# Sharing out the filler work over the four key tiles of a causal attention quad, and one staging tile of V for each layer

## The chip, the cores and the metric

The kernel runs on one core of one Trainium2 chip. The metric is the time of one execution on the device in microseconds (us); the time of a kernel is the median of several runs. A trace of one further, profiled execution shows what each engine did: TensorE (PE, with its weight loads as PEld), VectorE (DVE), ScalarE (ACT), GpSimd (POOL), and SyncE (SP), which only issues DMAs.

## The reference

Sixteen sequences (batches) of 512 tokens with 256 channels go through four attention layers, each with a layer norm ahead of it and a residual sum behind it. All have 16 heads of 16 channels. Layer 0 is causal attention with biases, layer 2 is attention with rotary positions, and layers 1 and 3 (the same weights twice) are attention in which tokens are split into two groups by a similarity; the split needs the minimum and maximum over all batches.

```python
def _L0_attn_a_ref(x, Wq, bq, Wk, bk, Wv, bv, Wo, bo):
    Q = x @ Wq.T + bq
    ...
    scores = jnp.einsum('bhqd,bhkd->bhqk', Qh, Kh) / jnp.sqrt(jnp.float32(HEAD_DIM))
    mask = idxs[None, :] <= idxs[:, None]
    scores = jnp.where(mask[None, None], scores, jnp.float32(-10000.0))
    attn = jax.nn.softmax(scores, axis=-1)
    ...
x = x + _L0_attn_a_ref(_layernorm(x, axis=-1), ...)
x = x + _L0_ffn_ref(_layernorm(x, axis=-1), ...)
x = x + _L0_attn_b_ref(_layernorm(x, axis=-1), ...)
x = x + _L0_ffn_ref(_layernorm(x, axis=-1), ...)
```

## The kernel before

**Tiling.** The work goes layer by layer (`PLAN`, line 62: causal "a", split "f", rotary "b", split "f"), in a layer batch by batch, in a batch by four *quads* of four heads (`quads`, line 587). A quad has four *key tiles* t = 0 to 3 of 128 keys. Queries and keys of a quad are read from HBM into one of five pairs of buffers (`load_quad`, line 574).

For one key tile PE makes the transposed scores (`products.score`, line 678: matmuls of line 687, and in the causal layer eight mask matmuls of line 698), ACT takes their exponentials (line 702), and PE multiplies them with V (`weigh`, line 706). In the causal layer a key tile t meets only the queries from 128 t on, so the scores are 512, 384, 256 and 128 columns wide for t = 0 to 3. Tiles 0 and 1 are the two *wide* ones: four exponentials each. In the narrow tiles 2 and 3 two score matrices share a bank of PSUM, and two exponentials do.

Some 20 half tiles ahead (`AHEAD`, line 63, `advance`, line 1056), the row maxima of a later quad are made: PE makes the scores once more (`maxima.score`, line 601, matmuls of line 610), and DVE takes their maxima (line 626). In the causal layer query tile t has 128 (t + 1) keys. As 20 half tiles are two quads and two tiles, the maxima of query tiles 2 and 3 (384 and 512 wide) stand beside key tiles 0 and 1, and those of query tiles 0 and 1 (128 and 256) beside key tiles 2 and 3.

**The other work.** Everything else is cut into steps, held in a list (`fill`) and put between the key tiles by a planner that runs when the kernel is built. The steps of layer 0's stretch are: `prep` of layer 0 for the batch after next (line 300; below called P: two normalizing steps n0 and n1, two steps v0 and v1 that make V, and q0, q1, k0, k1), the sums that a fully masked head needs (`masked`, line 836; m0 to m3), `tail` of the batch before (line 871; four divisions d0 to d3, two turns, two projections), and `prep` of layer 1 for batches whose tail is done (F: n0, n1, v0, v1, q0, q1, k0, `similar`, k1, `similarity`). A step has a planned cost on PE in ns (450 for a normalizing, dividing or turning step, 1380 for V and a projection, 1362 for q or k, 1750 for `similar`, 920 or 460 for `masked`) and a time before which it isn't due.

**How the order is set.** The order of PE's instructions is written out by hand: it is the order in which the planner emits them. The other engines' instructions are ordered by a scheduler; each engine and each DMA queue then works in its order and waits on semaphores. Each key tile (loop in line 1107) brings a fixed ration of planned time, `RATE` (line 1023), in `fill_in` (line 1026); `drain` (line 1006) takes the first step that is due and allowed, as long as the step costs no more than twice the credit in hand, and the credit is capped. At the third quad of a batch a `drain` without a credit (line 1095) runs whatever is needed until the batch before has been divided; at the end of a layer everything that is left is run (line 1127), because the split of the next layer needs all batches.

**V.** The steps v0 and v1 write the two halves of one of two staging tiles, `vst[b % 2]` (line 458), and a DMA on SP's queue sends the tile to HBM (line 482), from where `load_values` (line 581) reads it one layer later in the order of work. A flag lets only one `prep` of a layer at a time be past its normalizing steps (line 498), while one of layer 0 and one of layer 1 may run side by side.

Of the kernel before, what the change touches and what calls it, by code (L numbers as in the profile page):

```python
# [119 lines left out]
def hybrid_kernel(ctx: ExitStack, tc: tile.TileContext, a: dict, out: bass.AP):  # L120
# [24 lines left out]
    def small(name, dtype=F32):  # L145
        return ps_x.tile([P, S], dtype, tag="x", name=name)
# [84 lines left out]
    vst = []  # L231
    for i in range(2):
        t = res.tile([P, NT, VW], F32, tag=f"vst{i}", name=f"vst{i}")
# [3 lines left out]
    for i in range(2):  # L237
        t = res.tile([P, RW], FR, tag=f"rst{i}", name=f"rst{i}")
# [61 lines left out]
    def prep(layer, b, x):  # L300
# [154 lines left out]

        def values(u):

            v = vst[b % 2]
            xh, xl = st["xh"], st["xl"]
            ps = small(f"pv{n}_{u}")  # L460
            for k in range(2):
                t = 2 * u + k
                ts = slice(t * P, (t + 1) * P)
                seq = [(xl, wh), (xh, wl), (xh, wh)]
                for q, (xx, ww) in enumerate(seq):
                    for c in range(2):
                        nc.tensor.matmul(  # L467
                            ps[:, k * C : (k + 1) * C],
                            xx[:, c, ts],
                            ww[:, c, WV, :],  # L470
                            start=(q == 0 and c == 0),
                            stop=(q == 2 and c == 1),
                        )
            vo = v[:, 2 * u : 2 * u + 2, 0 : H * HV].rearrange("p t (h e) -> p t h e", e=HV)[:, :, :, 0:D]
            vi = ps.rearrange("p (t h d) -> p t h d", t=2, d=D)
            if kind == "a":
                bias = bv.rearrange("p (h d) -> p h d", d=D).unsqueeze(1).to_broadcast([P, 2, H, D])
                nc.vector.tensor_tensor(vo, vi, bias, ALU.add)
            else:
                nc.scalar.copy(vo, vi)  # L480
            if u == 1:
                nc.sync.dma_start(vd[b], v)
# [98 lines left out]
    def load_values(layer, b):  # L581
        t = p2.tile([P, NT, VW], F32, tag="v", name=f"v{layer}_{b}")
        nc.sync.dma_start(t, vd[b])
        V[layer, b] = t
# [251 lines left out]
    def masked(b):  # L836

        v = V[0, b]
        w_ = slice(0, H * HV)
        st = {}  # L840

        def start():
            nc.scalar.activation(EX[b], EX[b], AF.Exp)
            wv = p1.tile([P, 2, H * HV], F32, tag="wv", name=f"wv{b}")
            nc.gpsimd.tensor_tensor(wv[:, 1, :], v[:, 2, w_], v[:, 3, w_], ALU.add)
            nc.gpsimd.tensor_tensor(wv[:, 0, :], v[:, 1, w_], wv[:, 1, :], ALU.add)
            st["wv"] = wv
            X[b] = p1.tile([P, NT, H, HV], F32, tag="extra", name=f"xt{b}")

        def tile_(t):  # L850
            pf = small(f"sf{b}_{t}")
            nc.tensor.matmul(pf[:, w_], late["later"], v[:, t, w_], start=True, stop=(t == NT - 1))
            if t < NT - 1:
                rest = v[:, 3, w_] if t == 2 else st["wv"][:, t, :]
                nc.tensor.matmul(pf[:, w_], ones, rest, start=False, stop=True)
            nc.vector.tensor_tensor(
                X[b][:, t],
                pf[:, w_].rearrange("p (h e) -> p h e", e=HV),
                EX[b][:, t, :].unsqueeze(2).to_broadcast([P, H, HV]),
                ALU.mult,  # L860
            )

        yield (lambda: (b == 0 or (0, b - 1) in divided) and NG * b + NG - 1 in put), 0
        start()
        for t in range(NT):
            yield (POOL if t == 0 else 0), (460 if t == NT - 1 else 920)
            tile_(t)
        summed.add(b)
# [122 lines left out]
    def push(gen, rank):  # L991

        k = sum(s.rank <= rank for s in fill)
        fill.insert(k, Steps(gen, rank))
# [4 lines left out]
    def push_call(f, after=None):  # L999
        def gen():  # L1000
            yield (lambda: busy["prep"] == 0 and (not after or after in tailed)), 0
            f()

        push(gen(), 1)

    def drain(credit=None, until=None):

        while fill and not (until and until()):
            now = clock["now"]
            able = [s for s in fill if s.ready <= now and (s.next == 0 or banks[0] <= now) and s.open()]  # L1010
            if not able:
                if credit is not None:
                    return
                clock["now"] = min(max(s.ready, banks[0] if s.next else 0) for s in fill if s.open())
                continue
            s = able[0]
            if credit is not None:
                if s.next > 2 * max(0, credit["ns"]):
                    return
                credit["ns"] -= s.next  # L1020
            s.run()

    RATE = {0: 2100, 1: 1350, 2: 1250, 3: 700}
    credit = {"ns": 0}

    def fill_in(layer):

        credit["ns"] = min(credit["ns"] + RATE[layer], 2 * RATE[layer])
        drain(credit)

    def load_through(i):
        while loaded["n"] <= min(i, len(quads) - 1):
            j = loaded["n"]
            layer, b, g = quads[j]
            if (layer, b) not in prepared:
                drain(until=lambda: (layer, b) in prepared)
            if j >= NB:
                l_, b_, g_ = quads[j - NB]
                if PLAN[l_] == "f":
                    drain(until=lambda: (l_, b_, g_ // 2) in registered)  # L1040
            load_quad(j)
            loaded["n"] += 1

    def prep0(b, x=None):
        push(prep(0, b, load_x(0, b) if x is None else x), 2)
        busy["first"] += 1
        constant_rows(b)
# [27 lines left out]
    for i, (layer, b, g) in enumerate(quads):  # L1075
        kind = PLAN[layer]
        alone = b == 0 and g == 0 and (layer == 0 or kind == "f")
        held = kind != "f" and layer + 1 < len(PLAN) and PLAN[layer + 1] == "f"
        end = (layer + 1) * B * NG if held else len(quads)
        if b or g or layer:  # L1080
            load_through(min(end - 1, i + 4))
        if g == 0:
            load_values(layer, b)
            if kind == "f":
                first, second = registers(layer, b)
                push(first, 2)
                push(second, 2)
        if layer == 0 and g == (1 if b == 0 else 0):
            if b == 0:
                push_call(late_constants)  # L1090
            if b + 2 < B:
                prep0(b + 2)
        if g == 2 and i > NG:
            before = (layer, b - 1) if b else (layer - 1, B - 1)
            drain(until=lambda: before in divided)
        if kind == "a" and g == 1:
            push(masked(b), 2)
        if b == 0 and g == NG - 1 and layer + 1 < len(PLAN):
            push_call(lambda layer=layer: W.__setitem__(layer + 1, load_weights(layer + 1, False)))
        if b == 0 and g == NG - 2:  # L1100
            push_call(lambda layer=layer: WP.__setitem__(layer, load_weights(layer, True)), layer and (layer - 1, B - 1))
        if alone:
            advance((2 * NT) * i + AHEAD, 900)
        if i not in put:
            drain(until=lambda: i in put)
        score, weigh = products(i)
        for t in range(NT):
            for p in range(2):
                advance(min(2 * (NT * i + t) + p + 1 + AHEAD, 2 * NT * end))
                score(t, p)  # L1110
                clock["now"] += 230 + TURN
                if p == 0:
                    fill_in(layer)
                elif waiting:
                    waiting()
                    clock["now"] += 868 + TURN
                    waiting = None
            if t == 0 and g == 0 and (b > 0 or (layer > 0 and kind != "f")):
                push_tail(*((layer, b - 1) if b else (layer - 1, B - 1)))
            if i == 0:  # L1120
                load_through(i + 4) if t == NT - 1 else None
            waiting = lambda weigh=weigh, t=t: weigh(t)
        if kind != "f" and b == B - 1 and g == NG - 1 and layer + 1 < len(PLAN):
            waiting()
            waiting = None
            push_tail(layer, b)
            drain()
            split(layer + 1)
# [46 lines left out]
```

## Time and profile before

| | |
|---|---|
| median of 3 runs | 4260.31 us (4257.6 to 4260.97) |
| the profiled execution's own time | 4242.52 us |
| its span, first to last instruction | 4240.7 us |
| PE, DVE, ACT, POOL busy | 93%, 76%, 62%, 43% of the span |
| granted clock of PE, mean | 0.946 |
| first causal product / first product of layer 1 | 100.4 us / 1381.7 us |

A page of the profile gives, by part: (1) the busy time of each engine, (2) the span in 40 equal slices with the busy share of each engine in tenths and the clock that PE was granted, (3) DMA queues, (4) the chain of work that ended last, (5) the costliest groups of instructions with their mean time, and the idle time of the engine ahead of them with what ended it, (6) DMA issues. "L687" is line 687 of the kernel. The trace can also be asked for the busy times of all engines in chosen stretches, for who waited for whom, and for the instructions in order of time. A busy PE is not a PE at its peak: matmuls overlap, and short waits for a bank of PSUM disappear in their modelled ends.

### The profile page before, as it was taken

The page shows a single profiled execution, that of the slowest core. Times are in us where ns is not written, and L with a number is a line of the kernel's source. Part 1 is how long each engine was busy: PE and PEld are TensorE (multiplying, and loading weights), DVE is VectorE, ACT ScalarE, POOL GpSimd, SP SyncE. Part 2 cuts the span into 40 slices and gives each one's busy share as a digit, 9 for nine tenths or more (in the row PEclk, how much of TensorE's full clock was granted, in tenths as well). Part 3 has the DMA queues.
Part 4 walks back from the last instruction along what each step waited for, and adds up shares of the span by engine and source line. Part 5 has one row for each costly group of instructions (what it writes and reads, how often), then busy time and mean ns, then how long its engine had stood idle before and what let it go on. Part 6 is the DMA issues. An engine that isn't in the chain of part 4 may idle for free.

```text
span 4240.7 us, 79626 instructions
## 1 busy us (share of the span) xinstructions
PE 3937.4 (93%) x27440; PEld 2051.1 (48%) x27440; DVE 3207.0 (76%) x7488; ACT 2631.8 (62%) x5288; POOL 1820.8 (43%) x2421
## 2 busy tenths in 40 slices
PE   3899999999995999999999999999999599999999
PEld 2565656565553444444444444444444334444444
DVE  4676776667654888888888788888886389999996
ACT  1444454444452777777777667777777267777777
POOL 2124545354543256656665634444444412222221
PEclk6899999899996999999999999999999689999999
DMA  9556566666645345555554645455554623333331
GB/s 300 160 159 187 182 200 181 189 184 190 193 128 167 96 137 170 163 149 165 171 162 152 186 146 169 146 167 168 164 157 126 188 85 114 122 116 114 119 121 51
DMA packets 294722, 661.84 MB, mean 156 GB/s; under 512 B 51624, under 2 KB 90032, under 8 KB 294320
## 3 DMA queue, kind: packets, MB, share of 16 engines
q1 hardware_dynamic: 204080, 384.02, 28.9%
q0 software_dynamic: 90240, 272.73, 21.6%
q8 instruction: 219, 3.59, 0.3%
q14 instruction: 183, 1.50, 0.1%
HBM read 379.46 MB, written 298.06 MB: 160 GB/s over the span
## 4 chain that ended last, share of the span: by engine, by line
PE 72%; DVE 10%; DMA 7%; SPq 3%; ACT 3%; issue 3%; POOL 2%; ACTq 0%; DVEq 0%; POOLq 0%
PE po L713 19%; PE s L610 15%; PE t L687 11%; DVE mx L619 5%; PE pv L467 5%; PE pj L922 4%; PE pq L360 4%; DMA qd<-tq 3%; PE pk L360 3%; PE ot L884 2%; POOL nd L432 2%; DVE sc L626 1%; PE rs L759 1%; PE t L698 1%; SPq L568 1%
## 5 line engine op out<-in xcount | busy, mean ns | idle before, releaser
L702 ACT ACTIVATE e<-t 128x512 f32<-128x512 f32 (+2 forms) x3840 | 2017.6, 588 | 824.2 <-PE t L687 538.6
L619 DVE TENSOR_REDUCE mx<-s 128x1 f32<-128x512 f32 x3072 | 1944.4, 681 | 334.7 <-PE s L610 326.2
L610 PE MATMUL s<-ks,qs 52*128 52x512 f32 (+4 forms) x4096 | 1030.8, 481 | 92.3 <-DMA ks<-kd 78.1
L687 PE MATMUL t<-qs,ks 52*128 52x512 f32 (+4 forms) x4096 | 1000.2, 402 | 103.5 <-ACT e L702 35.5
L713 PE MATMUL po<-e,v 128*32 128x512 f32 (+1 forms) x8192 | 1031.1, 576 | 5.1 <-ACT o L729 3.9
L610 PEld LDWEIGHTS s<-ks,qs 48*128 48x128 f32 (+1 forms) x4096 | 429.9, 191 | 1085.7 <-ACT e L702 310.9
L687 PEld LDWEIGHTS t<-qs,ks 50*128 50x128 f32 (+1 forms) x4096 | 496.8, 191 | 302.3 <-DVE mx L619 102.6
L626 DVE CUSTOM_DVE_ANT_0 sc<-s,mask_s_bf 128x128 bf16<-128x128 f32 (+3 forms) x1024 | 497.7, 486 | 160.5 <-PE s L610 78.6
L577 POOL DMA_DIRECT2D qs<-qd x256 | 153.6, 601 | 811.5 <-PE t L687 530.7
L657 POOL DMA_DIRECT2D qs<-md x512 | 268.5, 529 | 543.7 <-DMA md<-ms 516.2
L432 POOL TENSOR_TENSOR nd<-nd,nhalf 128x16 f32<-128x16 f32 x120 | 346.1, 2902 | 22.5 <-DVE nd L423 22.5
L713 PEld LDWEIGHTS po<-e,v 128*32 128x32 f32 x8192 | 162.6, 109 | 271.9 <-issue 194.3
L309 POOL TENSOR_SCALAR xn<-x,nm,st 128x256 f32<-128x256 f32 x256 | 141.4, 557 | 117.7 <-PE xp L340 111.1
L698 PE MATMUL t<-mask_t_bf 64*128 64x128 bf16 x2048 | 189.4, 234 | 0.0
L380 POOL CAST tq<-yq 128x512 fp32r<-128x512 f32 x80 | 49.1, 613 | 267.9 <-DMA qd<-tq 92.5
L884 PE MATMUL ot<-ident,o 128*128 128x128 f32 x1024 | 148.2, 288 | 16.3 <-DVE tq L399 7.1
L577 POOL DMA_DIRECT2D ks<-kd x256 | 140.1, 548 | 52.1 <-issue 14.5
L729 ACT COPY o<-po 128x512 f32<-128x512 f32 x256 | 153.3, 599 | 7.4 <-PE po L713 7.0
L884 PEld LDWEIGHTS ot<-ident,o 128*128 128x128 f32 x1024 | 117.1, 146 | 47.8 <-DVE mx L619 10.1
L340 PE MATMUL xp<-ident,xn 128*128 128x128 f32 x512 | 89.1, 299 | 46.0 <-POOL xn L309 43.7
L930 DVE TENSOR_TENSOR x<-pj,x 128x512 f32<-128x512 f32 x128 | 87.1, 680 | 55.0 <-PE pj L922 50.5
L347 ACT CAST xh<-xp 128x512 fp32r<-128x512 f32 x128 | 76.0, 595 | 84.1 <-PE xp L340 83.9
(358 smaller groups left out, 4991.6 us busy)
## 6 DMA issues: line engine op xcount, KB each, us to landing
qs<-qd POOLq DMA_DIRECT2D x256, 512.0 KB, 4.5
ks<-kd POOLq DMA_DIRECT2D x256, 512.0 KB, 5.3
qd<-tq SPq DMA_DIRECT2D x256, 256.0 KB
kd<-tk SPq DMA_DIRECT2D x256, 256.0 KB
vd<-vst SPq DMA_DIRECT2D x64, 576.0 KB
v<-vd SPq DMA_DIRECT2D x64, 576.0 KB
qd<-tq SPq DMA_DIRECT2D x256, 128.0 KB
kd<-tk SPq DMA_DIRECT2D x256, 128.0 KB
```

The source lines that it names most:

```text
L360: nc.tensor.matmul(dst, ww[:, c, w, cols], xx[:, c, :], start=(k == 0 and c == 0), stop=(k == 2 and c == 1))
L432: nc.gpsimd.tensor_tensor(nd[:, 0, t], nd[:, 0, t], nhalf[:, t], ALU.pow)
L577: nc.gpsimd.dma_start(t, d[:, :, 2 * g : 2 * g + 2, :].rearrange("e r h s -> (e r) h s"))
L610: nc.tensor.matmul(st["ps"][e][:, (p % m) * end :][:, :end], q[r, p, t * P : (t + 1) * P], k[r, p, :end], start=True, stop=True,)
L619: nc.vector.tensor_reduce(st["mx"][:, e, p, t : t + 1], st["ps"][e], AX.X, ALU.max, negate=True)
L626: nc.vector.tensor_tensor_reduce(w, st["ps"][e][:, (i % m) * end :][:, :end], late["mask_s"][:, S - end :], 1.0, -3.0e38, ALU.add, ALU.max ...
L657: nc.gpsimd.dma_start(q[r : r + 2], d[:, e].rearrange("k j t p -> k j (t p)"))
L687: nc.tensor.matmul(ps[e], k[rows[e], p, t * P : (t + 1) * P], q[rows[e], p, q0:], start=True, stop=(kind != "a"),)
L698: nc.tensor.matmul(ps[e][:, :P], mk[:, 0], mk[:, 1], start=False, stop=(o == 1))
L702: st["exp", t] = nc.scalar.activation(e_[:, : m * w], st["ps"][e][:, : m * w], AF.Exp)
L713: mm = nc.tensor.matmul(st["po"][32 * j : 32 * j + 32, q0:], v[:, t, h * HV : h * HV + 32], E.pop((t, j)), start=(t == 0), stop=(t == NT - 1),
L884: nc.tensor.transpose(ps[:, g * P : (g + 1) * P], O[layer, b, g][:, t * P : (t + 1) * P], ident)
```

## The change

The ration of a key tile in layer 0 was 2100 for all four tiles; it becomes 1400 for the two wide ones and 2800 for the two narrow ones, which is 8400 for a quad as before. The cap on the credit is written in another way: what is left over is cut to one ration of the tile at hand before that ration is added. For equal rations (layers 1 to 3) this is the same as before. In layer 0 it cuts what is left to 1400 at a wide tile and to 2800 at a narrow one, where it was 2100.

The staging tile of V is chosen by layer and no longer by batch: all of layer 0's `prep` (and layer 2's) write the first tile, and all of layer 1's (and layer 3's) the second.

```diff
@@ values, line 458
-            v = vst[b % 2]
+            v = vst[layer % 2]
...
-    RATE = {0: 2100, 1: 1350, 2: 1250, 3: 700}
+    RATE = {0: (1400, 1400, 2800, 2800), 1: 4 * (1350,), 2: 4 * (1250,), 3: 4 * (700,)}
     credit = {"ns": 0}
 
-    def fill_in(layer):
-
-        credit["ns"] = min(credit["ns"] + RATE[layer], 2 * RATE[layer])
+    def fill_in(layer, t):
+
+        credit["ns"] = min(credit["ns"], RATE[layer][t]) + RATE[layer][t]
         drain(credit)
...
                 if p == 0:
-                    fill_in(layer)
+                    fill_in(layer, t)
                 elif waiting:
```

## The prediction

> **What bounds the kernel now.** I read the page's busy shares and slices first, to see in which layer an engine waits.
>
> ```profile
> span 4240.7 us, 79626 instructions
> ...
> PE 3937.4 (93%) x27440; PEld 2051.1 (48%) x27440; DVE 3207.0 (76%) x7488; ACT 2631.8 (62%) x5288; POOL 1820.8 (43%) x2421
> ...
> DVE  4676776667654888888888788888886389999996
> ...
> PEclk6899999899996999999999999999999689999999
> ```
>
> PE is nearly always busy, but in the causal layer (slices 1 to 11) its granted clock is mostly below full, and DVE is at six to seven tenths. Then the busy times by layer:
>
> ```profile
> 106.00:1272.00 1166.00, 1087.06 (x8869) 684.56 (x8868) 776.28 (x2872) 557.93 (x1180) 513.26 (x610) 0.92 0.59 177
> ...
> 1390.00:2327.00 937.00, 923.25 (x6311) 447.17 (x6314) 791.59 (x1481) 690.62 (x1373) 547.42 (x756) 1.00 0.50 152
> ```
>
> The columns are the stretch, its length, the busy times of PE, PEld, DVE, ACT and POOL, the granted clock, DMA share and GB/s. Layer 0 is the first row: PE idles 79 us and has a clock of 0.92; in layer 1 it idles 14 us at 1.00. In the order of instructions after the change, engine by engine, nothing differs once layer 0 is over. So only these 1166 us can move.
>
> Next, single key tiles. I took a tile from its first product (line 687) to that of the next tile, out of the timeline, and set beside each the steps that the planner puts there. Two tiles of each kind, the first without a step, the second with two steps of about 1.36 planned us each:
>
> ```profile
> 609.96:612.98 3.02, 2.77 (x26) 1.39 (x25) 2.52 (x11) 1.66 (x4) 0.57 (x2) 1.00 0.96 238
> 1176.02:1180.95 4.93, 4.93 (x50) 3.94 (x50) 3.67 (x17) 2.79 (x6) 2.26 (x7) 1.00 0.92 280
> 245.90:248.80 2.90, 2.90 (x27) 1.35 (x26) 2.47 (x8) 2.42 (x6) 1.48 (x3) 1.00 0.71 194
> 280.02:285.48 5.46, 5.46 (x44) 3.74 (x44) 4.51 (x15) 3.69 (x8) 3.39 (x6) 1.00 0.39 141
> 666.84:668.65 1.81, 1.81 (x27) 1.00 (x27) 1.58 (x9) 0.91 (x2) 0.00 (x0) 1.00 0.67 235
> 585.97:590.98 5.01, 5.01 (x50) 3.97 (x52) 3.73 (x16) 0.83 (x2) 0.00 (x0) 1.00 0.01 3
> 607.80:609.96 2.16, 2.16 (x28) 1.29 (x27) 1.60 (x10) 1.11 (x4) 1.77 (x3) 1.00 0.90 265
> 684.71:689.92 5.21, 4.83 (x51) 4.00 (x51) 1.94 (x10) 2.19 (x6) 0.57 (x1) 1.00 0.02 6
> ```
>
> Rows 1 and 2 are tile 0, 3 and 4 tile 1, 5 and 6 tile 2, 7 and 8 tile 3. Two steps lengthen tile 0 by 1.91 us and tile 1 by 2.56, but tile 2 by 3.20 and tile 3 by 3.05. **The same work is cheaper beside a wide tile.** The maxima say why:
>
> ```profile
> L626 DVE CUSTOM_DVE_ANT_0 sc<-s,mask_s_bf 128x512 bf16<-128x512 f32 x224 | 153.7, 686 | 32.3 <-PE s L610 14.2
> L626 DVE CUSTOM_DVE_ANT_0 sc<-s,mask_s_bf 128x384 bf16<-128x384 f32 x222 | 122.2, 550 | 37.1 <-PE s L610 22.8 <-PE t L698 0.5
> L626 DVE CUSTOM_DVE_ANT_0 sc<-s,mask_s_bf 128x256 bf16<-128x256 f32 x220 | 91.7, 417 | 32.9 <-PE t L687 19.8 <-PE s L610 5.6 <-PE po L713 0.5
> L626 DVE DVE_READ_ACCUMULATOR2_ANT mx<- 128x1 f32 x886 | 73.2, 83 | 0.0
> L626 DVE CUSTOM_DVE_ANT_0 sc<-s,mask_s_bf 128x128 bf16<-128x128 f32 x220 | 63.6, 289 | 31.1 <-PE s L610 21.3 <-DVE mx L626 0.2
> ```
>
> Four maxima with their reads stand beside each tile: 4 x (0.550 + 0.083) = 2.53 us beside tile 0, 4 x (0.686 + 0.083) = 3.08 beside tile 1, but 4 x (0.289 + 0.083) = 1.49 and 4 x (0.417 + 0.083) = 2.00 beside tiles 2 and 3. An empty wide tile lasts about as long as its maxima on DVE, and PE has room in it; a narrow one has less room.
>
> **The change part by part.** *The rations.* No step is added or dropped. In the planner's lists the planned time put into tiles 0, 1, 2, 3 of layer 0 goes from 124.8, 87.4, 77.6, 104.9 us to 93.6, 71.7, 108.8, 122.0: 46.9 us leave the wide tiles, 48.3 come to the narrow ones, and the 1.4 between is a k0 step that the unrationed drains lose. I price it in three ways from the tiles of layer 0 (one to twenty tiles for a median; without those at half clock, with unrationed drains, or in the first batch):
> - straight lines of tile length against planned time: slopes 0.69, 0.89, 1.13 and 1.05 us per planned us. -31.2 x 0.69 = -21.5; -15.7 x 0.89 = -14.0; +31.2 x 1.13 = +35.3; +17.1 x 1.05 = +18.0; less 1.4: **+16.4 us**;
> - medians by filling (tile 0: 3.02 empty, 3.90 with one step of 1.36, 4.95 with two; tile 1: 2.90, 4.29, 5.46; tile 2: 1.81, 3.57, 5.01; tile 3: 2.15, 3.30, 4.92), interpolated for every tile of both lists: -22.2, -12.8, +37.4, +20.3, less 1.4: +21;
> - a fit by kind of step (a projection of q or k: 1.05 wide, 1.57 narrow; V: 1.11 and 1.57): +10.
>
> I take the middle and keep 10 to 21.
>
> *Waits that move.* The lists repeat every three batches, before and after, with one unrationed drain in each (batches 4, 7, 10, 13 before; 3, 6, 9, 12 after), of the same eleven or so steps; those cancel. Three things don't:
> - `similar` and the k1 step behind it. k1 writes a tile of `parts`, of which there are two, and must wait until an earlier one has been sent; ACT stands in its queue, behind it the exponentials, behind these PE.
>
> ```profile
> ACT tk L401 <- DMA qd<-tq: 48.6, 14, 7.0
> ```
>
> ```profile
> 781.36 0.59 ACT L401 CAST tk<-pk 128x512 fp32r<-128x512 f32 x1 [7.04 <-DMA qd<-tq]
> ```
>
> The second line is batch 9: ACT waits 7.04 us, PE then idles 5.66 us (4.13 in batch 6). Where both steps stand in tile 1 of a batch's first quad it costs 4.7 us on the mean, where k1 stands one tile later 1.4: 6.1 in three batches. After, both stand in the narrow tile 2 of the first quad, twice in three batches. Bounds: nothing (at batch 7, tile 2 of the second quad, ACT waited 1.93 us and PE not at all, with other steps to run) to 5.66 each. In batch 9 the read of V (line 583) ran between the sends; tile 2 is later than that read, so I take 2.3 each, near the lower row: 4.6 - 6.1 = -1.5, four times: -6 us, bounds -24 to +21.
> - n1 with two turns in tile 1 of the second quad (batches 8, 11, 14): PE waits 2.2, 1.8, 1.3 us for POOL's normalized tile. After, the turns come later: -4 us, bounds -7 to 0.
> - three divisions come to tile 1 once in three batches. A division is 0.424 + 0.243 + 0.414 = 1.08 us on DVE; three on top of 3.08 us make 6.3, where the tile is priced at 4.3. +1.5 each, four times: +6 us, bounds 0 to +8.
>
> *V's staging tile.* It costs nothing: between a send of a staging tile (line 482) and the next write of the same one there were 12.4 us at the least; by layer it is 23.7 us in the drain at a layer's end and 41 or more before it, and a `prep`'s q and k projections lie between. ACT or DVE would wait if the send took longer. What the tile by layer does allow is a V of layer 0 between the halves of one of layer 1, as the new order has it.
>
> *Sum.* 16.4 - 6 - 4 + 6 = **+12 us**: 4242.5 becomes about 4255 in a profiled execution. The median of the runs lies 17.8 us above the profiled one, so I add the 12 to it: **4273 us**.
>
> **The clock.** PE's clock was halved 23 times in layer 0, 177 us in all, each a multiple of about 3.4 us long, mostly after 1.3 to 5.7 us of idle time. I count as many halvings after. [...]
>
> **The rivals.** *A: the waits and the halvings go (faster).* Place: ACT's wait in front of k1 and what follows. Price: idle 4.13, 5.66, 4.34 us in batches 6, 9, 12 and 3.99 in batch 2, with half-clock stretches of 6.8, 10.2, 6.8 and 6.8 us behind them, half of which is lost (15.3): 33.4 us; the n1 waits of batches 8, 11, 14 with their stretches (3.4 each): 5.3 + 5.1. Together 44. If more than 16 to 22 of it goes, the change gains; if all goes, 16 - 44 = -28: 4232 us. For it: some wide tiles with two or more steps have DVE at 95% (5.0 of 5.3 us with two projections and n1 in tile 0 of batch 6), and the rations thin these out. Against: `similar` and k1 are still in one tile, and now twice in three batches.
> *B: k1 waits in full (slower still).* 5 us each instead of 2.3 is +22, with one halving more in three batches (3.4 lost): +14; 12 + 22 + 14 = +48: 4308 us. For it: behind a narrow tile 2 there are few exponentials in PSUM for PE to go on with.
> *C: no change.* PE's own time for the steps is the same in every tile, and PE is busy 93%. If my price differences are only short waits that come elsewhere, it is 4260 us. Against: tile lengths differ by over a microsecond with the same steps.
>
> **How the numbers follow.** Forecast (+5 to +30) 0.42, A 0.25, C 0.18, B 0.15. The range leaves out the far ends of A and B: 4236 to 4304 us; the forecast's own is 4265 to 4290. This kernel's runs can tell about 0.2%, 8.5 us. Faster by more: A, 0.25. Within: C and a little of the forecast, 0.20. Slower: 0.55.
>
> **What would show it.** Right: layers 1 to 3 as long as before; two steps beside tile 2 still cost about 3 us, empty wide tiles still last about 3; ACT waits at line 401 in total near 48 us; layer 0 about 12 us longer. Wrong: full narrow tiles of 4 us, or ACT's wait for the sends far below 40 us and a clock in layer 0 well above 0.92.

## The result, and the profile after

The median went from 4258.95 us (4245.61 to 4260.97, four runs) to 4289.09 us (4284.48 to 4294.22, four runs). The ratio is 1.0078, with a 95% interval of 1.0053 to 1.0102: the change costs about 30 us, 0.8%. The profiled execution took 4284.48 us, where that of before took 4242.52; these two are 42 us apart, so an account of them holds some 12 us that the medians don't.

These are the span, PE's busy time, DVE's slices and PE's granted clock from the page of the kernel after:

```profile
span 4282.3 us, 79673 instructions
...
PE 3959.2 (92%) x27440; PEld 2054.9 (48%) x27440; DVE 3208.1 (75%) x7488; ACT 2628.5 (61%) x5288; POOL 1815.9 (42%) x2421
...
DVE  4676666666662888888888777888787289999996
...
PEclk6898998989997899999999999999999789999999
```

PE has the same 27,440 matmuls and is busy 22 us longer; the other engines' busy times have not moved by more than 5 us. So no engine got work. The clock digits differ from before's in single slices, most of them in layer 0, and say little; the layers say more. These are the busy times in the stretches of layers 0 and 1 (columns as in the prediction; layer 0 is now longer, so its stretch is too):

```profile
106.00:1308.00 1202.00, 1107.45 (x8855) 691.36 (x8853) 776.65 (x2866) 553.65 (x1177) 512.09 (x609) 0.91 0.58 172
1418.00:2364.00 946.00, 931.90 (x6334) 451.03 (x6336) 796.95 (x1489) 695.05 (x1383) 546.46 (x755) 0.99 0.50 151
```

From the first causal product to the last, layer 0 went from 1169.9 to 1207.7 us. The other stretches (layer 0 to 1, layers 1, 2 and 3, and what lies between) changed by +6 us at the most (layer 2), and by +4 together. The whole loss is in layer 0, as the prediction had it. There, with nearly the same products in it, PE is busy 20 us longer and idles 16 us longer (94.6 us of 1202 where it was 78.9 of 1166; with the wait ahead of the layer's first product, 110.6 and 97.1), and the time at half clock went from 180 to 228 us.

Three tiles of after, in the stretches' columns: an empty tile 0, a tile 2 with two steps, an empty tile 2:

```profile
542.50:545.51 3.01, 2.77 (x27) 1.39 (x25) 2.51 (x11) 1.66 (x4) 2.51 (x3) 1.00 0.80 202
633.30:638.69 5.39, 5.39 (x42) 2.47 (x40) 1.89 (x11) 1.45 (x3) 0.18 (x1) 1.00 0.79 196
617.49:619.30 1.81, 1.81 (x26) 1.00 (x28) 1.63 (x8) 0.83 (x2) 0.00 (x0) 1.00 0.00 0
```

They last what such tiles lasted before (3.02, 5.01 and 1.81 us). The second is `similar` and k1 in tile 2 of a first quad; they cost 3.1 planned us, so they stand a little above two projections. An empty tile 2 under the half clock looks like this:

```profile
598.58:601.83 3.25, 3.25 (x26) 1.62 (x26) 1.28 (x9) 1.09 (x2) 0.00 (x0) 0.50 0.49 161
```

The same 26 matmuls take 3.25 us where they took 1.81, and PE shows no idle time at all: in such a tile the clock alone costs 1.44 us.

What PE waited for in layer 0 of after (total, times, longest; us):

```profile
PE t L687 <- ACT e L702: 17.0, 12, 3.2
PE xp L340 <- POOL xn L309: 13.1, 4, 4.3
PE xp L340 <- DVE tk L402: 12.0, 4, 3.7
PE ot L884 <- DVE tq L399: 11.0, 4, 3.3
...
PE s L610 <- DVE tk L402: 7.4, 4, 2.4
```

The same of before:

```profile
PE t L687 <- ACT e L702: 25.8, 13, 5.7
PE t L687 <- DVE tk L402: 7.2, 5, 1.9
PE ot L884 <- DVE tq L399: 7.1, 4, 2.2
...
PE xp L340 <- POOL xn L309: 5.4, 3, 2.2
```

Before, PE waited 25.8 us for exponentials, 5.4 for the normalized tile (line 309), and 19.1 for DVE behind one of the parts of q and k (lines 399 and 402). After it is 17.0, 13.1 and 33.0. The waits for DVE are, at least in part, ACT's waits for sends in another place: DVE makes the second part after ACT made the first, and in after it waits for ACT ahead of lines 399 and 402 (30.5 us ahead of the part of q at line 399 and 31.4 ahead of that of k at line 402, between 175 and 1300 us). ACT's own waits for them in layer 0 of after:

```profile
ACT tk L398 <- DMA qd<-tq: 44.5, 18, 4.6
ACT tk L401 <- DMA qd<-tq: 27.7, 11, 3.1
ACT tq L398 <- DMA kd<-tk: 24.2, 4, 6.9
```

And the two of line 398 before:

```profile
ACT tk L398 <- DMA qd<-tq: 36.8, 19, 5.1
...
ACT tq L398 <- DMA kd<-tk: 11.4, 2, 5.7
```

The wait of k1 (line 401) fell from 48.6 to 27.7 us, but those in layer 0's own `prep` (line 398) rose from 36.8 and 11.4 to 44.5 and 24.2. With the smaller ones it is 98 us in all before, 103 after.

**Where the 38 us are.** For each of the 256 tiles of layer 0 I took the length that the prediction's straight lines give it (3.19 us and 0.69 for each planned us in tile 0, 3.09 and 0.89 in tile 1, 2.10 and 1.13 in tile 2, 1.98 and 1.05 in tile 3; unrationed steps at their planned cost) and looked at what the tile lasted beyond it, apart for tiles in which the clock was halved and tiles in which it wasn't:

| kernel | layer 0 | lines | rest, tiles at full clock | rest, tiles with half clock | half clock, us |
|---|---|---|---|---|---|
| before | 1170.3 | 1061.7 | +5.5 | +103.2 | 180 |
| after | 1208.0 | 1078.0 | -13.5 | +143.5 | 228 |
| difference | +37.7 | +16.3 | -18.9 | +40.3 | +47 |

Tiles in which the clock was halved hold 40 us more, the others 19 us less. The split between the two columns is rough: the kernel before with three tiles for the parts (below) has before's order on PE, and its tiles at full clock stand at -13.8, 19 us under before's. So the -18.9 doesn't show that the price of the moved steps, 16.3, was given back. A second reckoning, for batches 1 to 15, says more: their length went from 1093.5 to 1129.2 us, PE's idle time from 70.4 to 83.6, the half clock from 153.8 to 198.0; length less idle time less half of the half clock is 946.2 before and 946.7 after. So idle time and half clock account for 35 of these 36 us. But over the fourteen profiles of this document that remainder goes from 939 to 962 us, and it differs by 12 us between after and another kernel with the same order on PE (`after_xn_dve`); a price of some 10 us isn't excluded. Beside the profiled execution of `v_only` (4253.02 us, before's order on PE), batches 1 to 15 of after are 29 us longer, with 11 us more idle time and 32 us more half clock.

### The profile page after: what moved, and what is told of

Read it like the earlier page. It is cut to its first block, busy times and chain, and to the rows that moved or that the text cites. A ratio compares the mean times of both kernels' runs of the same rounds, so it can differ in the third digit from the quotient of the medians.

```text
span 4282.3 us, 79673 instructions
## 1 busy us (share of the span) xinstructions
PE 3959.2 (92%) x27440; PEld 2054.9 (48%) x27440; DVE 3208.1 (75%) x7488; ACT 2628.5 (61%) x5288; POOL 1815.9 (42%) x2421
## 4 chain that ended last, share of the span: by engine, by line
PE 71%; DVE 10%; DMA 7%; issue 4%; SPq 3%; ACT 3%; POOL 2%; DVEq 0%; ACTq 0%; POOLq 0%
PE po L713 19%; PE s L610 15%; PE t L687 11%; DVE mx L619 5%; PE pv L467 4%; PE pj L922 4%; PE pq L360 4%; DMA qd<-tq 3%; PE pk L360 3%; PE ot L884 2%; DVE sc L626 2%; POOL nd L432 2%; PE rs L759 1%; PE pa L903 1%; SPq L568 1%
## 5 line engine op out<-in xcount | busy, mean ns | idle before, releaser
L687 PE MATMUL t<-qs,ks 52*128 52x512 f32 (+4 forms) x4096 | 997.4, 404 | 84.9 <-DMA qs<-md 30.7
L687 PEld LDWEIGHTS t<-qs,ks 50*128 50x128 f32 (+1 forms) x4096 | 496.9, 192 | 279.4 <-DVE mx L619 101.2
L729 ACT COPY o<-po 128x512 f32<-128x512 f32 x256 | 153.8, 601 | 6.3 <-PE po L713 5.9
L402 DVE TENSOR_TENSOR tk<-pk,tk 128x512 fp32r<-128x512 f32 x64 | 44.0, 688 | 117.3 <-ACT tk L401 102.7
```

What stands on the lines that cost most here:

```text
L687: nc.tensor.matmul(ps[e], k[rows[e], p, t * P : (t + 1) * P], q[rows[e], p, q0:], start=True, stop=(kind != "a"),)
```

## The experiments

Every ratio is to the kernel before in runs on the same chip; where two experiments are set beside each other, the ratio of their ratios is given, with the interval that the two of them make together (the root of the sum of the squares). Layer 0 is from a single profiled execution each; two kernels with the same order of PE (before and `v_only`) differ by 8 us in it, so differences below 10 us in a layer are not read.

### V's staging tile alone

The kernel before, with the one line of V changed:

```diff
-            v = vst[b % 2]
+            v = vst[layer % 2]
```

> The kernel before with only V's staging tile chosen by layer. Price theory (the same steps cost more beside narrow tiles) and wait theory (the loss is waits of PE and the half clock behind them) both expect no change, ratio 0.998 to 1.002, and the span of layer 0 (first to last product) at 1170 us within 5. The rival that V's tile carries the loss expects +30 us and ACT or DVE waiting for the send of V in front of lines 478 and 480.

4254.57 us, 0.9991 [0.9977, 1.0005]. In before's order the tile by layer costs nothing that can be seen. The new order wasn't run without it, but in its trace neither ACT nor DVE waits for the send of V ahead of lines 478 and 480. So the loss is put down to the rations.

### The rations the other way round

The kernel after, with the larger rations at the wide tiles:

```diff
-    RATE = {0: (1400, 1400, 2800, 2800), ...}
+    RATE = {0: (2800, 2800, 1400, 1400), ...}
```

> The kernel after with the rations turned round: 2800 beside the wide tiles, 1400 beside the narrow ones. Planned time by tile is 129.7, 108.8, 66.2, 88.4 us. Price theory: by the straight lines of the kernel before, 6 us less than before and 22 less than after; so about 4253 us, ratio 0.9985. Wait theory: similar and k1 stand in one tile only in three batches instead of eight, so the waits behind them shrink too, by up to 20 us of idle and half clock: 4235 us. A rival that any uneven ration hurts expects it slower than before by 10 to 30 us.

4255.68 us, 0.9998 [0.9983, 1.0014]. The straight lines promise 6 us less for this kernel, 0.15%, which the interval allows. In its profiled execution, the slowest of its runs (4270.07 us), it has less idle time than before in batches 1 to 15 (60.6 us for 70.4) and more half clock (180.9 for 153.8), which pull against each other.

### k1 set later

In both kernels, `prep` of layers 1 and 3 lets at least 4000 planned ns pass between `similar` and k1:

```diff
             similar()
-            yield 0, 1362
+            yield TWO, 1362
             parts("k", 1)
```

> The kernel before with the k1 step of layers 1 and 3 due no sooner than 4 us of planned time after similar. Both no longer stand in one tile. Price theory: 0 us (straight lines give -0.2). Wait theory: the waits of batches 6, 9, 12 (14 us of idle, 12 us lost at half clock) and some behind one-tile-later k1 go: -15 to -30 us, 4230 to 4245.

> The kernel after with the same k1 delay. Price theory: the straight lines give 14.5 us over before, so about 4274 us, and near 4289 if waits elsewhere stay as in after. Wait theory alone: the eight waits behind similar and k1 (19 us idle) and their half-clock stretches go, so it comes back to before or below: 4250 to 4262 us. With both: 14 us above the kernel before with the same delay.

The kernel before with it: 4238.77 us, 0.9955 [0.994, 0.9969], but layer 0 is as long as it was (1168.3 us); what it gains is in layer 2 (948.7 us for 960.7, with 10 us of half clock for 27). The time lies where the wait theory had it, but not by the waits of layer 0 that this theory named. The kernel after with it: 4199.96 us, 0.986 [0.984, 0.988], faster than both kernels by far and than any of the theories had it, and here the gain is in layer 0: 1128.0 us for 1207.7. The stretch of the first 1164 us shows it (9006 matmuls, where before had 8869 in 1166 us):

```profile
106.00:1270.00 1164.00, 1086.64 (x9006) 694.25 (x9003) 787.62 (x2902) 562.42 (x1196) 536.88 (x631) 0.94 0.62 183
```

This kernel carries the rations of after, with two wide tiles thinned out and all. By the straight lines its layer 0 should be 14.5 us longer than before's; it is 42 us shorter. So the price of a step beside a narrow tile does not decide the time. With k1 later, the planner's order has a period of one batch (about 70 us each) instead of three, and only one unrationed drain (batch 3) in place of four. That made three candidates for the loss: the unrationed drains, the pairs of `similar` and k1, and the waits for sends.

### No drains, no pairs

Four more kernels change the rations so that the planner's list has other drains and pairs. The edits to the kernel after:

```diff
+ even2700:          RATE = {0: (2700, 2700, 2700, 2700), ...}
+ even2700_k1late:   the same, and yield 4000, 1362 ahead of k1
+ uneven1300_k1late: RATE = {0: (1300, 1300, 2600, 2600), ...}, and yield 4000, 1362 ahead of k1
+ uneven1500:        RATE = {0: (1500, 1500, 3000, 3000), ...}
```

> Even rations of 2700 in layer 0, no k1 delay. The list has no unrationed drain before the layer's end, but similar and k1 stand in one tile (tile 0 of the fourth quad) in ten batches. Straight lines: +2 us. Drain theory: layer 0 at 1125 to 1140, the whole about 4215 to 4225. k1 theory: the pairs are more than before, so layer 0 at 1170 to 1190 and the whole at 4258 or above. Price theory alone: 4260.

> Even rations of 2700 with the k1 delay: neither drains nor pairs, and by the straight lines 8 us cheaper than the delayed kernel with uneven rations (1065.7 against 1074.2 us). Price theory on top of drain or k1 theory: layer 0 at 1118 to 1124, the whole 4190. If the price of a step beside a narrow tile is no real cost: 4200 within 5. If uneven rations themselves help once the waits are gone (the stated purpose of such a change): slower than 4200, 4215 or more.

> The kernel after with the k1 delay and smaller uneven rations (1300 and 2600). The planner's list has unrationed drains in batches 3, 6, 9 and 12 as in after, but similar and k1 stand together in none of the batches up to 14. It undoes the one difference between after and the delayed kernel of 4200 us that the delay isn't named for: the drains. Price theory (straight lines): layer 0 17 us above before's 1170, so 1187. k1 theory: without the pairs layer 0 falls to 1130 to 1145, as in the kernel of 4200 us. Drain theory (each unrationed drain costs some 10 us in waits and half clock behind it): layer 0 stays at 1170 to 1200, and the whole at 4240 to 4275, as layer 2 gains about 15 us by the delay of its own k1.

> The kernel after with 1500 and 3000 in place of 1400 and 2800, nothing else. The list has no unrationed drain before the layer's end and no pair of similar and k1 in a tile, with still more planned time beside the narrow tiles (straight lines: 23 us above before, 7 above after). Drain or k1 theory: layer 0 at 1130 to 1150 and the whole at 4220 to 4235, although it differs from after by 7% in the rations. Price theory alone: layer 0 7 us longer than after's 1208, 4295.

| kernel | drains | pairs in one tile | us | ratio | layer 0, us |
|---|---|---|---|---|---|
| even2700 | none | ten batches, in tile 0 | 4252.97 | 0.9992 [0.9975, 1.0008] | 1163.1 |
| even2700_k1late | none | none | 4235.79 | 0.995 [0.9933, 0.9967] | 1172.6 |
| uneven1300_k1late | four | four batches, in the drains | 4238.52 | 0.9961 [0.9944, 0.9978] | 1175.2 |
| uneven1500 | none | none | 4285.77 | 1.0061 [1.0044, 1.0079] | 1205.1 |

The last row ends both stories as the whole cause. `uneven1500` has neither a drain nor a pair and is as slow as after. (The four pairs of `uneven1300_k1late` stand in the planner's list, inside the unrationed drains; the expectation had none.) All forecasts of a layer 0 under 1150 us failed. The drain theory came out for the layer 0 of `uneven1300_k1late` (1170 to 1200), but `even2700_k1late`, without a drain, is as long; for `even2700` price theory and k1 theory were near, for `uneven1500` price theory alone. PE's largest waits in `uneven1500`:

```profile
PE t L687 <- ACT e L702: 29.7, 14, 3.9
PE ot L884 <- DVE mx L626: 10.5, 11, 1.2
```

(The view is that of PE's waits in the first 1164 us.) And the kernel with four drains (`uneven1300_k1late`) is level with the one that has none (`even2700_k1late`): 1.0011 +- 0.0024. As their rations differ too, this doesn't price a drain by itself.

### A third tile for the sends

The parts of q and k get three tiles instead of two. The room is taken from a tile of exponentials and from another buffer; PE's order of instructions is the same to the last one as without it:

```diff
-        pool("p4", 2),
-        pool("pe", 9),
+        pool("p4", 3),
+        pool("pe", 8),
...
-                    EX[b] = p3.tile([P, NT, H], F32, tag="ex", name=f"ex{n}")
+                    EX[b] = p2.tile([P, NT, H], F32, tag="ex", name=f"ex{n}")
```

> The kernel before with three tiles of parts in place of two (room from one buffer of the exponentials, eight in place of nine, and one of the ex tiles, two in place of three). PE's order is the same to the instruction. A projection step then waits for the send of three steps earlier. Wait theory (ACT stands in front of lines 398 and 401 for a send, PE idles behind it, the clock is halved behind that): ACT's 99 us of waits for the sends in layer 0 fall below 40, idle time by some 20 us, half clock by 40 us or more, time by 30 to 45 us: 4215 to 4230. If those waits are harmless: 4258 within 10. If eight buffers of exponentials are too few: slower in all layers.

> The kernel after with the same three tiles of parts and unchanged order on PE. Wait theory: ACT's 91 us of waits for the sends fall below 40, and with them the idle time and the halvings, so that half clock in layer 0 is at most 180 us; 4235 to 4255, and the distance to the other kernel with three tiles is 0 to 15 us. Price theory: the distance stays at 16 us or more, whatever the waits do. If the halvings come from thin PE work in the near-empty wide tiles and not from these waits: distance near the old 30, half clock still 40 us above its neighbour's.

> The fastest kernel so far (uneven rations, k1 delayed, 4200 us) with three tiles of parts. Its ACT still waits for sends. Wait theory: another 10 to 25 us, 4175 to 4190. If its half clock (123 us in layer 0) is of other causes: 4195 to 4200.

Before with it: 4200.26 us, 0.9865 [0.9842, 0.9888]. After with it: 4229.19 us, 0.9936 [0.9913, 0.9958]. Both gain 1.4% by their ratios, so the waits for the two tiles are dear; ACT's waits for sends in layer 0 fall to 41 and 51 us. In the profiled executions layer 0 gains 36 us (1133.7 for 1169.9) and 31 (1176.9 for 1207.7), the rest of the kernel some 20 in each. But the distance between the two stays: 29 us, a ratio of 1.0072 +- 0.0032, where it was 1.0078. It is again idle time (60 and 79 us in layer 0) and half clock (133 and 207 us). **The waits for sends are not what the change added.** What takes their place is read from PE's waits in layer 0, first of before, then of after, each with three tiles:

```profile
PE xp L340 <- POOL xn L309: 13.6, 4, 3.4
PE s L610 <- DMA ks<-kd: 9.7, 2, 9.3
PE t L687 <- DVE mx L626: 6.8, 18, 1.1
PE s L610 <- DVE tk L399: 5.7, 4, 2.0
```

```profile
PE xp L340 <- POOL xn L309: 27.7, 5, 6.0
PE s L610 <- DVE tk L399: 11.7, 4, 3.7
```

The waits for the normalized tile (line 309) and for the part of k (line 399) are double in the kernel after, and that for the row maxima on their way into the queries (`PE t L687 <- DMA qs<-md`) is 10.0 us for 3.3. The fastest kernel so far went the other way: `after_k1late` with three tiles is 4238.62 us, 0.9964 [0.995, 0.9979], 1.05% slower than without by the ratios. Its largest wait of PE in layer 0, and POOL ahead of one of these waits, in batch 11 (start, length, engine, line, operation, tiles, shape, count):

```profile
PE xp L340 <- POOL xn L309: 70.8, 11, 9.7
```

```profile
954.34 11.53 POOL L432 TENSOR_TENSOR nd<-nd,nhalf 128x16 f32<-128x16 f32 x4
965.87 1.10 POOL L309 TENSOR_SCALAR xn<-x,nm,st 128x256 f32<-128x256 f32 x2
```

Four powers of 2.9 us each, of the step `similarity`, whose result isn't needed until the layer ends, stand ahead of the two normalized tiles that PE waits for, here in eleven batches. They stand there in before and after with three tiles too.

### The normalized tile off POOL's queue

In the kernel after it is the same in batches 4, 7, 10 and 13, in before in batches 8, 11 and 14, where PE waits less. POOL's timeline of after in batch 13:

```profile
1107.18 11.53 POOL L432 TENSOR_TENSOR nd<-nd,nhalf 128x16 f32<-128x16 f32 x4 [2.70 <-DVE nd L423]
1118.72 1.09 POOL L309 TENSOR_SCALAR xn<-x,nm,st 128x256 f32<-128x256 f32 x2
```

POOL works without a pause here, and PE waits 4.3 us. The last experiment lets DVE make the normalized tiles of layers 0 and 1; PE's order is unchanged again:

```diff
-            nc.gpsimd.tensor_scalar(
+            (nc.vector if layer < 2 else nc.gpsimd).tensor_scalar(
                 xn, x[:, t, :], st["nm"][:, t : t + 1], st["s"][:, t : t + 1], ALU.add, ALU.mult
             )
```

> The kernel after, with the normalized tiles of layers 0 and 1 (line 309) computed by DVE and no longer by POOL; PE's order of instructions is the same to the last one. In the kernel after, PE waits in layer 0 for POOL's normalized tile for 13.1 us (four waits of about 3 us, in batches 4, 7, 10 and 13; in the kernel before 5.4 us), because the four powers of line 432, 11.5 us in a row, stand ahead of the tile in POOL's queue. A half-clock stretch of 6.8 us lies around each of the four waits. Theory 1, the part of the loss that the change added comes by this wait: the 13.1 us go, and with them up to four stretches, half of which is lost (13.6 us): 4289 less 13 to 27 = 4262 to 4276 us, and the idle time of PE in layer 0 falls from 110 to 97 us or less. Theory 2, it is the order as a whole, and a wait that is taken away in one place comes back in another (for ACT's sends of the k tiles, or for DVE, which now has 128 tiles more to make): 4281 to 4297 us, with PE's idle time in layer 0 still above 105 us and its half clock near 215 us.

4276.00 us, 1.006 [1.0039, 1.008]. The runs of before beside it had a median of 4249.01, so the kernel is 27 us slower than before, where after is 30 us slower. PE's waits in its layer 0:

```profile
PE t L687 <- ACT e L702: 13.9, 13, 2.1
PE xp L340 <- DVE tk L402: 11.5, 4, 3.3
PE ot L884 <- DVE tq L399: 9.8, 4, 3.1
...
PE t L687 <- DVE mx L626: 8.1, 14, 2.4
PE s L610 <- DVE tk L402: 5.7, 4, 1.7
PE pa L903 <- DVE mx L626: 5.4, 6, 3.7
```

The wait for POOL is gone, and PE's idle time in layer 0 fell from 110.6 to 98.5 us, close to the 97 of theory 1; DVE, which has more to do, is now late with its maxima (3.1 us in all in front of products of line 687 in after, 8.1 here; 1.0 in front of line 903, 5.4 here). By the time as a share of before, the kernel stands within the interval of after's ratio, and above the 1.001 to 1.004 that theory 1 amounts to, by a little. Beside after it is a ratio of 0.9982 +- 0.0032, 8 us less, give or take 14. Half clock in layer 0 fell from 228 to 199 us in the profiled executions, where theory 2 had it stay. So this wait may carry a part of the loss; the runs don't show it clear of noise, and that it carries most of it is not borne out.

## Why the prediction was right, and where it was wrong

**Right.** Only layer 0 moved. The tile of V costs nothing that can be seen. The sign is right and the range holds the time, 1 us inside its upper end of 4290; 4273 was forecast, and the loss is 30 us where the sum had 12. The tiles shown above, at full clock and with like fillings, last what they lasted before. That the range holds the time is in good part luck: the sum took the loss for the price of the moved steps, let the waits take 4 us off it and the clock nothing, and the profiles show the loss as idle time and half clock.

**The price of the rations, +16.4.** By kind of tile the change did what the lines say: tile 0 -23.6 us (forecast -21.5), tile 1 -4.1 (-14.0), tile 2 +40.2 (+35.3), tile 3 +25.1 (+18.0). But these sums hold the idle time and the half clock too. By the second reckoning above, idle time and half clock account for 35 of 36 us, which leaves the price little room, within some 10 us. In other pairs a part of it may be left (between `even2700` and `uneven1500` the lines differ by 21.3 us and the full-clock rest by -8.0), and `after_k1late` overrules it altogether. A fit over all fourteen profiles, batches 1 to 15, gives 0.29 us of length for each us of the lines (give or take some 0.17), next to 0.52 for each us of half clock and 0.62 for each us of idle time (5 us of scatter). So the price reads as a mean over a layer's circumstances more than as a property of a step.

**The waits, -6 - 4 + 6.** In the planner's lists `similar` and k1 share a tile in eight batches before the layer's end, before as after, and so not more often after. k1's wait at line 401 fell more than forecast (to 27.7 us, where about 48 was expected), and came back at line 398: the sends of one ring are awaited by whoever writes next. PE's wait at n1, forecast to fall by 4, rose by 7.7. The +6 for three divisions wasn't measured by itself. The first two were read step by step, each wait at the place where the steps stood before; but here a wait belonged to an engine's queue or to a ring of tiles, and appeared where something of it was needed next (20.9 us less at line 401, 20.5 more in the two waits of line 398). The sum of PE's idle time in batches 1 to 15 rose by 13 us, where the two terms for waits had -10.

**The clock, "as many halvings after".** This is the step that failed most. The equal count was my estimate and no run shows it: there were 23 halvings with 177 us, there are 31 with 222 (counted from 106 us on). In batches 1 to 15, the waits of 1 us and more are nearly as many as before (28 for 26), but beside 26 of them a halving begins (from just before the wait to 7 us after its start), where it was 18 of 26. What this count leaves out is the length of the waits: 17 of after's last 2 us or more, where it was 8 (10 in `v_only`). In the fourteen profiles a halving begins beside 125 of 126 waits of 2 us and more, beside 50 of 67 from 1.5 to 2 us, and beside 55 of 100 from 1 to 1.5. So the longer waits, and the halvings with them, are what the forecast lacked.

**The rivals.** C held that PE's own time for the steps is the same in every tile; the remainder of the second reckoning (946.2 and 946.7 us) agrees with it within its scatter, but the waits and the clock made the end. Of B, more halvings came, without its cause: k1's wait did not grow. A's waits are worth about what I gave them (44 us in layer 0, with the n1 waits): with a third tile layer 0 is 36 and 31 us shorter, and the whole kernel 1.4%, as other layers gain too; but these waits didn't go with the change.

**What stays open.** The rations that favour the narrow tiles cost 0.7 to 0.8% in three pairs of kernels: before and after, the same two with three tiles for the parts, and `even2700` and `uneven1500` (1.0069 +- 0.0024). In a pair with k1 later the same rations gain: 0.986 against 0.9955, a ratio of 0.9905 +- 0.0025. With drains and pairs gone, or the waits for sends cut by half, the loss stayed, and other waits stood in their place; for the wait for POOL, the noise leaves it open. That the loss is idle time and half clock is shown by the profiles, within some 10 us. The longer waits go with the halvings in three pairs: 17 waits of 2 us and more for 8; 13 for 7 with three tiles; and with k1 later 4 in the kernel that gains, 9 in the other. In `uneven1500` and `even2700` they don't (8 and 7, with 195 and 133 us of half clock in batches 1 to 15). Why these rations lengthen the waits, most of the time, is not shown. That PE is less busy around a wait where wide tiles are thin is a guess. The sign that the expectation of `after_parts3` gave for it came (29 us apart, and 74 us more half clock in layer 0), but longer waits would give the same sign.

## What to carry to other kernels

Where PE's order is written out by hand, a price per step from a regression over tiles was worth little here: look for the queues and rings of tiles that PE waits for, count their waits as a whole and not by the step that happened to meet them, and expect a freed wait to come back at the next one. Give a staging ring one tile more before shifting steps around: here it was worth 1.4%, about twice what the sharing out of the steps cost (though not in every order: with k1 later, it cost 1%). And measure several orders, as neither the prices nor the single waits foretold which was best: the rations that cost 0.8% were, with one step set later, part of the fastest kernel (4199.96 us, level with before and three tiles at 4200.26).

## What the runs showed of the hardware

In these traces half clock came mostly after short idle times. In batches 1 to 15 of after there are 29 halvings, and three waits longer than 3.4 us; the stretches of half clock last 3.4, 6.8, 10.2, 13.7 or 20.5 us. Most halvings follow 1 to 3 us of idle time: in 21 of the 29, PE idles that long in the 3.4 us ahead. In each of the fourteen profiles all changes of the clock in batches 1 to 15 lie on one grid of 3.413 us, to within 3 ns. Of the steps of this grid at full clock, all 91 with 2 us or more of idle PE are followed by half clock, 119 of 154 with 1.1 to 2 us, and 65 of 3520 with less than 0.8 us. In the 20.5 us of half clock from 585.9 us of after, PE is busy throughout in five of the six steps, and the clock stays at half.

Over the fourteen profiles, the length of batches 1 to 15 is fitted by 968 us + 0.53 of the half clock + 0.67 of the idle time, to 6 us, so a us of half clock goes there with about half a us of length; by the half clock alone it is fitted to 10 us (992 us + 0.66 of it). The empty tile 2 shown above took 3.25 us at a clock of 0.50 and 1.81 at 1.00.

On POOL one power of 128x16 elements took 2.89 us in after (line 432), where two normalized tiles of 128x256 took 1.09 us together (line 309).
